# A four-layer network on one core: product with C on GpSimd, state sums by accumulating transfers, softmax reciprocals through DRAM

## The chip, the core and the metric

The kernel runs on one core of a Trainium2 chip. The metric is the device time of one execution in microseconds. Before the change it is 3715.52 us, the median of three runs (3714.67 to 3716.05). The profile is of one execution with a span of 3718.9 us.

Engine names are those of the profile: PE is TensorE (matrix products), PEld its weight loads, DVE is VectorE, ACT is ScalarE, POOL is GpSimd, and SP is SyncE, which issues nearly all transfers.

## What is computed

Four images of 128 channels and 64 x 64 pixels pass through four layers; N = 4096 is the number of pixels.

```python
# layer 0: attention over the pixels, 16 channels for q and k
energy = q^T k;  attn = softmax(energy);  x = gamma * (v @ attn^T) + x
# layer 1: two 3x3 convolutions with 4-bit weights and activations, residual
# layer 2: selective scan over the 4096 pixels, 256 inner channels, 16 states
def step(h, inp):
    dt_t, B_t, C_t, x_t = inp
    dA = exp(dt_t[..., None] * A)
    h = dA * h + dt_t[..., None] * B_t[:, None, :] * x_t[..., None]
    y = einsum('bdn,bn->bd', h, C_t)          # sum over the 16 states
    return h, y
# ys = scan(step) + xc * D; y = ys * silu(z); x = silu(group_norm(y @ W_out)) + x
# layer 3: attention over the pixels, 64 channels, softmax, output projection, residual
```

The change touches the sum over states in layer 2 (`y = einsum(h, C)`) and the division of both attentions by their softmax sums.

## The kernel before

All four layers run interleaved, so that each engine finds work in one layer while another waits. Each piece of work is a Python generator that yields `op(engine, time, needs...)` before it issues an instruction. `Order.run` (line 80) repeatedly takes the generator whose next operation could begin earliest by the planned times, adds a small penalty by rank (line 95), and lets it issue. The result is one fixed order of instructions for every engine and for the transfer queue. `lag` is the planned time from the issue of a transfer to its landing. An entry marked `port` is planned so as not to overlap another such entry, since DVE and GpSimd can hold each other up. The real waits on the chip are semaphores that the framework puts in; the plan only fixes the order.

**Attention (layers 0 and 3).** There are eight stages of 64 steps: layer 0 of images 0, 1 and 2, then layer 3 of image 0, layer 0 of image 3, and layer 3 of images 1, 2 and 3. In one step `t` PE computes energies `e` of 1024 keys against 256 queries (line 494), ACT takes the exponentials `p` (line 513), and PE multiplies them with the values into `us[:, 0]` (line 571) and with ones into `us[:, 1]`, which gives the softmax sums (line 591). In the first eight column blocks and in the last stage DVE adds the exponentials first (`acc`, line 535) and PE sums only the result. Four steps make one block of 256 queries in a single PSUM bank, `us`. PE opens each bank with products of zero (line 553), so that all later products may accumulate.

After two blocks (512 queries, a chunk; 64 chunks in all) `parts` lets ACT copy values and sums out (lines 617 and 619), and `finish` divides: four products with `sel4` turn the sums into columns (line 638), DVE takes reciprocals (line 647), four products with the identity spread them over all partitions (line 651), and DVE multiplies (line 659). In layer 0 the result is added into the padded image `xpad` (line 664); in layer 3 it is projected (line 670), added to the residual `o` loaded by `residual`, and written out (line 677).

**Scan (layer 2).** An image is cut into 8 pieces of 512 pixels; 32 pieces `g` with 16 states `n` make 512 steps `m`. Every tile of a step is 128 partitions x 1024 values (two halves of 256 channels). For each step:

- SP fetches the rows of B and C for state `n` from DRAM, broadcast to all partitions (`bc`, line 978, 512 KB, three buffers);
- ACT computes the decays `da` into PSUM (line 991, two halves);
- DVE multiplies `ud` with B into `hs` (line 1018, three buffers), runs two scans in place (line 1026), and then, after the next step's product with B, multiplies the state with C (`readout`, line 1008);
- ACT saves the last column for the next piece (`hlast`, line 1001);
- GpSimd adds the product to `y` (line 1043). After 16 states it multiplies `y` with the gate `sz` (line 1047), and PE projects it into `yo` (line 905).

`yo` of a whole image stays in SBUF in eight buffers until its group norm is known; then `x2` is formed in place and written to DRAM (line 969), from where layer 3 reads it (`stage_input`, line 378).

Of the kernel before, what the change touches and what calls it, by code (L numbers as in the profile page):

```python
# [8 lines left out]
F32 = mybir.dt.float32  # L9
# [11 lines left out]
P = 128  # L21
W = 64
N = W * W
TB = 512
# [23 lines left out]
class Order:  # L48
# [7 lines left out]
    def __init__(self):  # L56
        self.clock = dict.fromkeys(("PE", "ACT", "DVE", "POOL", "SP"), 0.0)
        self.marks = {}
        self.chains = []
        self.table = None  # L60
        self.bank = 0.0
        self.port = 0.0
        self.end = (0.0, None)

    @staticmethod
    def op(engine, time, *needs, bank=False, table=None, port=False, lag=0.0):
        return engine, time, needs, bank, table, port or engine == "POOL", lag
# [9 lines left out]
    def release(self):  # L77
        self.bank = self.end[0]

    def run(self):  # L80
        while self.chains:
            best = None
            for item in self.chains:
                engine, time, needs, bank, table, port, lag = item[3]
                if any(k not in self.marks for k in needs) or (bank and self.bank is None):
                    continue
# [3 lines left out]
                if bank:  # L90
                    start = max(start, self.bank + self.HOP)
# [8 lines left out]
            engine, time, needs, bank, table, port, lag = item[3]  # L100
# [3 lines left out]
            if bank:  # L104
                self.bank = None
# [29 lines left out]
def conv_seq_kernel(ctx: ExitStack, tc: tile.TileContext, i: dict, out: bass.AP):  # L135
# [47 lines left out]
    zero = const.tile([P, 1], BF16, tag="zero", name="zero")  # L183
    nc.gpsimd.memset(zero, 0.0)
# [49 lines left out]

    sel4 = const.tile([P, 1], F32, tag="sel4", name="sel4")
    nc.gpsimd.memset(sel4, 0.0)
    for k in range(4):
        nc.gpsimd.memset(sel4[32 * k : 32 * k + 1, :], 1.0)
# [126 lines left out]
    def stage_input(s):  # L365

        layer, b = stages[s]
        for c in range(NTB // 2):
            need = [("x2", b, 2 * c), ("x2", b, 2 * c + 1)] if layer == 3 else []
            need += [("sums", s * NS - 2 + c // 2), ("exp", s * NS - 1, 1)]  # L370
            yield op("SP", 0.1, *need, lag=3.5)
# [10 lines left out]
    def operands(s):  # L382
# [19 lines left out]
        def high_low(o, g, key, bias, low, n):  # L402
# [3 lines left out]
            yield op("ACT", 0.2 + n * 1e-3, (*key, "in"), *lows[c - 1 : c])  # L406
            h = att.tile([P, 2 * TB], F32R, tag="h", name="h", bufs=1)
            nc.scalar.activation(h[:, 0:n], g, AF.Identity, bias=low[1], scale=low[0])
            yield op("DVE", 0.06 + n * 1.2e-3)
            nc.vector.scalar_tensor_tensor(o, g, bias, h[:, 0:n], ALU.add, ALU.subtract)  # L410
            mark(*key)
# [4 lines left out]
        for c in range(NTB // 2):  # L416
# [9 lines left out]
            if layer == 0:  # L426
                order.add(1, high_low(o, flat(g), key, bq0r, low0[0], 2 * TB))
            else:
                order.add(1, copy(o, flat(g), key, 1.2))
# [24 lines left out]
            if layer == 0:  # L454
                mark(*key, "in")
                o = jts[s][:, c * TB : (c + 1) * TB]
                order.add(1, high_low(o, g[:, 0, :], key, bk0r, low0[1], TB))
# [15 lines left out]
            order.add(1, copy(o, flat(g) if layer == 0 else g, key, 1.2))  # L473
        return freed + lows

    def energies():
# [5 lines left out]
        for s, (layer, b) in enumerate(stages):  # L482
            if s:
                order.add(1, stage_input(s))
# [37 lines left out]
    def accumulations():  # L522
        for t in filter(added, range(len(stages) * NS)):
            k, q = divmod(t, NQ)
            for h in range(2):
# [6 lines left out]
                if q == 0:  # L532
                    accs[k] = att.tile([P, 2, 2, CB], F32, tag="acc", name="acc", bufs=1)
# [4 lines left out]
    def products():  # L538
        mark("evict", -1)
        for t in range(len(stages) * NS):  # L540
# [3 lines left out]
            for h in range(2):  # L544
                need = [("evict", k0 - 1)] if q == 0 and h == 0 else []
                time = (1.93 if layer == 0 else 0.95) + (0.3 if need else 0.0)
                yield op("PE", time, ("exp", t, h), *need)
                if need:

                    us = uss[k0] = ps_u.tile([P, 2, CB], F32, tag="us", name="us")  # L550
                    d = P if layer == 0 else 32
                    for m in range(P // d):
                        nc.tensor.matmul(
                            flat(us)[m * d : (m + 1) * d, :],
                            lhsT=w3[:, 0, m * d : (m + 1) * d],
                            rhs=zero.to_broadcast([P, TB]),
                            start=True,
                            stop=False,
                        )
                for k in range(2 * h, 2 * h + 6):  # L560
# [9 lines left out]
                    for rows, cols in tiles:  # L570
# [4 lines left out]
                            start=False,  # L575
# [26 lines left out]
    def parts():  # L602


        for s, (layer, b) in enumerate(stages):
            for c in range(NTB):
                k0 = s * NCB + 2 * c
                us = ss = None
                for k in range(k0, k0 + 2):
                    need = [("parts", s * NTB + c - 2)] if s or c > 1 else []  # L610
                    yield op("ACT", 0.45, ("sums", (k + 1) * NQ - 1), *need)
                    if us is None:
                        us = att.tile([P, TB], F32, tag="us", name="us", bufs=2)
                        ss = att.tile([P, TB], F32, tag="ss", name="ss", bufs=2)
                    cols = slice((k - k0) * CB, (k - k0 + 1) * CB)
                    scale = gam0 if layer == 0 else 1.0
                    nc.scalar.activation(us[:, cols], uss[k][:, 0, :], AF.Copy, scale=scale)
                    yield op("ACT", 0.4)
                    nc.scalar.copy(ss[:, cols], uss.pop(k)[:, 1, :])
                    mark("evict", k)  # L620
                if layer == 3:
                    order.add(1, residual(b, c))
                order.add(0, finish(s, c, us, ss))

    def residual(b, c):
        n = NTB * b + c
        yield op("SP", 0.1, *([("out", n - 1)] if n else []), lag=2.5)
        outs[b, c] = o = att.tile([P, TB], F32, tag="o", name="o", bufs=1)
        nc.sync.dma_start(out=o, in_=x2s[b][c])
        mark("res", n)  # L630

    def finish(s, c, us, ss):
        layer, b = stages[s]
        n = 2 * NTB * b + (0 if layer == 0 else NTB) + c
        yield op("PE", 0.65, bank=True)
        sc = gtile("sc")
        for k in range(4):
            nc.tensor.matmul(  # L638
                sc[:, k : k + 1],
                lhsT=ss[:, k * P : (k + 1) * P],  # L640
                rhs=sel4,
                start=True,
                stop=True,
            )
        yield op("DVE", 0.18)
        r = rall[:, 4 * n : 4 * n + 4]
        nc.vector.reciprocal(r, sc[:, 0:4])

        yield op("PE", 1.15)
        for k in range(4):  # L650
            nc.tensor.matmul(  # L651
                sc[:, k * P : (k + 1) * P],
# [897 lines left out]
```

## Time and profile before

| quantity | value |
|---|---|
| time, median of three runs | 3715.52 us |
| span of the profiled execution | 3718.9 us |
| mean TensorE clock granted | 0.967 |
| scan steps on DVE, first to last start | 242.9 to 3361.4 us |
| PE `us` products with values (L571), busy | 1521.7 us |
| PE energies (L494), busy, two row groups | 534.6 and 196.5 us |
| PE softmax sums with ones (L591), busy | 469.9 us |
| PE `sc` sums (L638), `sc` broadcasts (L651), zero products (L553), busy | 72.7, 74.5, 48.3 us |
| DMA queue of SP, share of 16 engines' span | 34.7% |

The span in 40 equal slices, busy tenths of each, shows how the work is spread; the scan fills slices 3 to 36:

```profile
PE   5999979989989999999888999999899989998998
DVE  3369999999999999899988999999789888893333
ACT  3467767777787777777677767767777777774443
POOL 0014434444434444344433444443344444441000
PEclk8999999999999999999999999999999999999999
DMA  2023334333443334443443333343434444331000
```

Transfers, with size and median time from issue to landing:

```profile
bc<-bc_d SPq DMA_DIRECT2D x512, 512.0 KB, 4.9
x_in<-in_x SPq DMA_DIRECT2D x16, 512.0 KB, 4.8
xpad<-in_x SPq DMA_DIRECT2D x32, 256.0 KB, 3.4
x_d<-yo SPq DMA_DIRECT2D x32, 256.0 KB, 2.3
x_in<-x_d SPq DMA_DIRECT2D x16, 512.0 KB, 6.0
o<-x_d SPq DMA_DIRECT2D x32, 256.0 KB, 5.4
out<-o SPq DMA_DIRECT2D x32, 256.0 KB, 2.2
bc_d<-xd SPq DMA_DIRECT2D x64, 32.0 KB, 1.7
```

### The profile page before, as it was taken

The page shows a single profiled execution, that of the slowest core. Times are in us where ns is not written, and L with a number is a line of the kernel's source. Part 1 is how long each engine was busy: PE and PEld are TensorE (multiplying, and loading weights), DVE is VectorE, ACT ScalarE, POOL GpSimd, SP SyncE. Part 2 cuts the span into 40 slices and gives each one's busy share as a digit, 9 for nine tenths or more (in the row PEclk, how much of TensorE's full clock was granted, in tenths as well). Part 3 has the DMA queues.
Part 4 walks back from the last instruction along what each step waited for, and adds up shares of the span by engine and source line. Part 5 has one row for each costly group of instructions (what it writes and reads, how often), then busy time and mean ns, then how long its engine had stood idle before and what let it go on. Part 6 is the DMA issues. An engine that isn't in the chain of part 4 may idle for free.

```text
span 3718.9 us, 70774 instructions
## 1 busy us (share of the span) xinstructions
PE 3406.0 (92%) x29874; PEld 2235.8 (60%) x29879; DVE 3104.3 (83%) x2944; ACT 2513.0 (68%) x3656; POOL 1314.1 (35%) x568
## 2 busy tenths in 40 slices
PE   5999979989989999999888999999899989998998
PEld 3776656666666666655545666665555545565665
DVE  3369999999999999899988999999789888893333
ACT  3467767777787777777677767767777777774443
POOL 0014434444434444344433444443344444441000
PEclk8999999999999999999999999999999999999999
DMA  2023334333443334443443333343434444331000
GB/s 70 1 53 96 91 103 100 90 95 92 117 102 97 94 87 95 112 107 101 106 114 102 89 91 92 88 112 87 107 95 108 119 91 108 101 104 63 13 19 17
DMA packets 203658, 327.82 MB, mean 88 GB/s; under 512 B 50609, under 2 KB 53441, under 8 KB 203329
## 3 DMA queue, kind: packets, MB, share of 16 engines
q1 hardware_dynamic: 196384, 322.09, 34.7%
q8 instruction: 236, 3.87, 0.4%
q10 hardware_dynamic: 6944, 1.10, 0.2%
q14 instruction: 94, 0.76, 0.1%
HBM read 304.27 MB, written 18.87 MB: 87 GB/s over the span
## 4 chain that ended last, share of the span: by engine, by line
PE 61%; DVE 21%; ACT 10%; issue 5%; DMA 2%; ACTq 0%; SPq 0%; DVEq 0%
PE us L571 25%; PE e L494 14%; DVE hs L1026 9%; PE us L591 7%; DVE hs L1018 4%; DVE hs L1008 3%; PE conv L686 2%; ACT da L991 2%; ACT p L513 2%; PE xh L775 2%; PE sc L651 2%; PE yo L905 1%; PE sc L638 1%; PE proj L465 1%; PE proj L423 1%
## 5 line engine op out<-in xcount | busy, mean ns | idle before, releaser
L1043 POOL TENSOR_TENSOR y<-y,hs 128x1024 f32<-128x1024 f32 x512 | 1215.3, 2374 | 2050.1 <-DVE hs L1008 2033.6
L571 PE MATMUL us<-p,v 128*32 128x256 f32 (+1 forms) x12288 | 1521.7, 389 | 128.3 <-ACT p L513 128.1
L571 PEld LDWEIGHTS us<-p,v 128*32 128x32 f32 (+1 forms) x12288 | 1009.0, 138 | 550.1 <-ACT p L513 153.5
L513 ACT ACTIVATE p<-e 128x1024 f32<-128x1024 f32 x1024 | 1002.0, 1019 | 383.2 <-PE e L494 255.5
L1026 DVE TENSOR_TENSOR_SCAN hs<-da,hlast,hs 128x512 f32<-128x512 f32 x896 | 1102.3, 1264 | 45.5 <-ACT da L991 45.2
L991 ACT ACTIVATE da<-dt,amat 128x512 f32<-128x512 f32 x1024 | 701.1, 690 | 266.8 <-DVE hs L1026 263.0
L1008 DVE TENSOR_TENSOR hs<-hs,bc 128x1024 f32<-128x1024 f32 x512 | 666.9, 1303 | 34.7 <-ACT hlast L1001 33.8
L1018 DVE TENSOR_TENSOR hs<-ud,bc 128x1024 f32<-128x1024 f32 x512 | 656.9, 1283 | 0.0
L494 PE MATMUL e<-it,v 64*128 64x256 f32 x4096 | 534.6, 402 | 9.2 <-ACT p L513 8.2
L494 PEld LDWEIGHTS e<-it,v 64*128 64x128 f32 x4096 | 386.9, 193 | 155.6 <-issue 89.6
L591 PE MATMUL us<-p,ones 128*32 128x256 f32 x7040 | 469.9, 385 | 0.0
L591 PEld LDWEIGHTS us<-p,ones 128*32 128x32 f32 x7040 | 202.4, 110 | 183.6 <-issue 64.5
L535 DVE TENSOR_TENSOR acc<-p 128x1024 f32<-128x1024 f32 x24 | 29.4, 1225 | 225.4 <-PE us L591 192.6
L494 PEld LDWEIGHTS e<-it,j 64*128 64x128 f32 x2048 | 141.5, 190 | 101.9 <-issue 69.1
L494 PE MATMUL e<-it,j 64*128 64x256 f32 x2048 | 196.5, 310 | 5.1 <-ACT p L513 3.4
L1001 ACT COPY hlast<-hs 128x2 f32<-128x2 f32 x448 | 85.4, 191 | 130.9 <-DVE hs L1026 129.1
L535 DVE TENSOR_TENSOR acc<-p,acc 128x1024 f32<-128x1024 f32 x96 | 117.4, 1223 | 61.6 <-ACT p L513 58.1
L1026 DVE TENSOR_TENSOR_SCAN hs<-da,hs 128x512 f32<-128x512 f32 x128 | 149.9, 1204 | 8.6 <-ACT da L991 8.5
L775 PEld LDWEIGHTS <-w 128*128 128x128 bf16 x576 | 51.4, 98 | 98.3 <-issue 54.3
L775 PE MATMUL xh<-x,w 128*128 128x512 fp8e4 x384 | 95.3, 385 | 1.1 <-ACT sz L798 0.4
L1047 POOL TENSOR_TENSOR y<-y,sz 128x1024 f32<-128x1024 f32 x32 | 95.2, 2976 | 2.5
L465 PE MATMUL proj<-L_conv_wvT,x_in 128*128 128x128 f32 (+1 forms) x512 | 67.7, 288 | 22.9 <-DVE it L410 13.2
(162 smaller groups left out, 2617.3 us busy)
## 6 DMA issues: line engine op xcount, KB each, us to landing
bc<-bc_d SPq DMA_DIRECT2D x512, 512.0 KB, 4.9
x_in<-in_x SPq DMA_DIRECT2D x16, 512.0 KB, 4.8
xpad<-in_x SPq DMA_DIRECT2D x32, 256.0 KB, 3.4
x_d<-yo SPq DMA_DIRECT2D x32, 256.0 KB, 2.3
x_in<-x_d SPq DMA_DIRECT2D x16, 512.0 KB, 6.0
o<-x_d SPq DMA_DIRECT2D x32, 256.0 KB, 5.4
out<-o SPq DMA_DIRECT2D x32, 256.0 KB, 2.2
bc_d<-xd SPq DMA_DIRECT2D x64, 32.0 KB, 1.7
```

Source lines behind the costliest of these rows:

```text
L465: nc.tensor.matmul(to[:, k * d : (k + 1) * d], lhsT=x[:, k // 4, k % 4 * P : (k % 4 + 1) * P], rhs=wv, start=True, stop=True,)
L494: nc.tensor.matmul(e[k % 4 // 2][:, k % 2, k // 4, :], lhsT=jts[s][row : row + D3, col : col + P], rhs=its[s][row : row + D3, c * CB : (c ...
L513: nc.scalar.activation(p, es[t][h], AF.Exp)
L535: nc.vector.tensor_add(accs[k], ps[t, h], other)
L571: nc.tensor.matmul(us[rows, 0, :], lhsT=vts[s][:, 8 * q + k, cols], rhs=ps[t, h][:, k % 2, k // 4, :], start=False, stop=False,)
L591: nc.tensor.matmul(us[32 * m : 32 * m + 32, 1, :], lhsT=ones[:, 0:32], rhs=term, start=False, stop=q == NQ - 1 and k >= len(terms) - 4,)
L775: nc.tensor.matmul(g, lhsT=w3[:, k // len(rhs), lhs[k % len(rhs)] : lhs[k % len(rhs)] + P], rhs=x[:, rhs[k % len(rhs)]], start=(k == 0), s ...
L991: nc.scalar.activation(da, live["in", g][0][:, h, :], AF.Exp, scale=amat[:, h, n : n + 1])
L1008: nc.vector.tensor_mul(hs, hs, bcs.pop(m)[:, 1:2, :].to_broadcast([P, 2, TB]))
L1018: nc.vector.tensor_mul(hs, ud, bcs[m][:, 0:1, :].to_broadcast([P, 2, TB]))
L1026: nc.vector.tensor_tensor_scan(hs[:, h, :], das.pop((m, h)), hs[:, h, :], hlast[:, n, h : h + 1] if g % NTB else 0.0, ALU.mult, ALU.add,)
L1043: nc.gpsimd.tensor_tensor(y, y, hss.pop(m), ALU.add)
```

## The change

**Product with C and sum over states.** GpSimd, not DVE, multiplies the state with C. It then issues a transfer that adds the product into one of three tiles in SBUF: `y`, `odd1` or `odd2`, by `n % 3`. The transfers of states 1 and 2 overwrite `odd1` and `odd2`, all others add. After 16 states DVE adds `odd1` and `odd2` into `y`, and GpSimd multiplies with the gate as before. `hs` and `bc` have four buffers each instead of three. DVE is to be relieved of one of its two products per step.

**Softmax reciprocals.** ACT copies values and sums out in one instruction. The sums go to DRAM (`s_d`), come back as 128 partitions x 4 x 4 (`st`), DVE reduces and inverts them, the reciprocals go to DRAM (`r_d`) and come back broadcast to all partitions (`rb`). DVE multiplies with `rb`. PE's products with `sel4` and the identity go away. `rb` shares one buffer with the residual `o`, whose load now waits for the product.

**Opening of the bank.** The first product of a bank carries the start flag, so the products of zero go away.

**Buffers.** To make room, `yo` goes to DRAM and comes back in two batches of four, `h` shares the buffer `sp` with the softplus, and `acc` shares `odd1`.

**Plan.** The planned transfer times are raised (for example `bc` from 5.0 to 7.5 us, an accumulating transfer is planned at 8.2), and the ranks of the generators are set anew. In the plan a GpSimd operation no longer takes the port by default, since issuing a transfer does not.

```diff
@@ class Order
-        return engine, time, needs, bank, table, port or engine == "POOL", lag
+        return engine, time, needs, "bank" if bank else lock, table, port, lag
@@ accumulations
-                    accs[k] = att.tile([P, 2, 2, CB], F32, tag="acc", name="acc", bufs=1)
+                    accs[k] = pair("acc", "odd1", 1).rearrange("p a (b c) -> p a b c", b=2)
@@ products
-                    d = P if layer == 0 else 32
-                    for m in range(P // d):
-                        nc.tensor.matmul(
-                            flat(us)[m * d : (m + 1) * d, :],
-                            lhsT=w3[:, 0, m * d : (m + 1) * d],
-                            rhs=zero.to_broadcast([P, TB]),
...
-                            start=False,
+                            start=q == 0 and k < (1 if layer == 0 else 2),
@@ parts
-                    yield op("ACT", 0.45, ("sums", (k + 1) * NQ - 1), *need)
+                    yield op("ACT", 0.6, ("sums", (k + 1) * NQ - 1), *need)
...
-                    nc.scalar.activation(us[:, cols], uss[k][:, 0, :], AF.Copy, scale=scale)
-                    yield op("ACT", 0.4)
-                    nc.scalar.copy(ss[:, cols], uss.pop(k)[:, 1, :])
+                    nc.scalar.copy(us[:, :, k - k0, :], uss.pop(k))
@@ finish
-        yield op("PE", 0.65, bank=True)
-        sc = gtile("sc")
...
-        nc.vector.tensor_mul(us, us, sc)
+        yield op("SP", 0.1, ("evict", 2 * k + 1), lag=5.0)
+        s_d = dram.tile([4, TB], F32, tag="s_d", name="s_d")
+        nc.sync.dma_start(out=s_d, in_=us[0:P:32, 1, :])
+        us = us[:, 0, :]
+        mark("s_d", k)
+        yield op("SP", 0.1, ("s_d", k), lag=7.0)
+        st = att.tile([P, 4, 4], F32, tag="st", name="st", bufs=2)
+        nc.sync.dma_start(out=st, in_=s_d.rearrange("g (p e) -> p g e", e=4))
+        mark("st", k)
+        yield op("DVE", 0.3, ("st", k))
         r = rall[:, 4 * n : 4 * n + 4]
+        nc.vector.tensor_reduce(r, st.rearrange("p g e -> p e g"), AX.X, ALU.add)
+        nc.vector.reciprocal(r, r)
+        yield op("SP", 0.1, lag=5.0)
+        r_d = dram.tile([TB], F32, tag="r_d", name="r_d")
+        nc.sync.dma_start(out=r_d.rearrange("(p e) -> p e", e=4), in_=r)
+        mark("r_d", k)
+        yield op("SP", 0.1, ("r_d", k), *([("end", k - 1)] if k else []), lag=8.0)
+        rb = att.tile([P, TB], F32, tag="o", name="rb", bufs=1)
+        nc.sync.dma_start(out=rb, in_=r_d.unsqueeze(0).to_broadcast([P, TB]))
...
+        nc.vector.scalar_tensor_tensor(us, us, scale, rb, ALU.mult, ALU.mult)
@@ output
-            yo = big.tile([P, TB], F32, tag="yo", name="yo", bufs=NTB)
+            yo = big.tile([P, TB], F32, tag="yo", name="yo", bufs=4)
...
+            nc.sync.dma_start(out=yo_d[c], in_=yo)
...
+                    x2.append(big.tile([P, TB], F32, tag="yo", name="x2", bufs=4))
+                    nc.sync.dma_start(out=x2[-1], in_=yo_d[k])
@@ fetches
-            need = [("c", m - 3)] if m > 2 else []
-            yield op("SP", 0.1, ("bc_d", g), *need, lag=5.0)
+            need = [("c", m - 4)] if m > 3 else []
+            yield op("SP", 0.1, ("bc_d", g), *need, lag=7.5)
@@ scans
-            if m:
-                yield op("DVE", 1.22, ("last", m - 1), port=True)
-                readout(m - 1)
@@ additions becomes readouts and gates
-            yield op("POOL", 2.36, ("c", m), ("y", g))
-            nc.gpsimd.tensor_tensor(y, y, hss.pop(m), ALU.add)
+            yield op("POOL", 2.6, ("s", m, 1), ("last", m), port=True)
+            nc.gpsimd.tensor_tensor(
+                hs, hs, bcs.pop(m)[:, 1:2, :].to_broadcast([P, 2, TB]), ALU.mult
+            )
...
+            need = [("y", g)] if n == 0 else [("add", m - 3)] if n > 2 else []
+            if n in (1, 2) and g:
+                need.append(("summed", g - 1, n))
+            yield op("POOL", 1.2, *need, lag=8.2)
...
+            nc.gpsimd.dma_start(
+                out=sums[g][n % 3],
+                in_=hss.pop(m),
+                accum_op=ALU.bypass if n in (1, 2) else ALU.add,
+            )
...
+                yield op("DVE", 1.22, ("add", m - 4 + k), ("add", m - 1), port=True)
+                nc.vector.tensor_add(y, y, sums[g][k])
@@ ranks
-            (3, scans()),
-            (3, additions()),
-            (3, fetches()),
+            (1, scans()),
+            (6, readouts()),
+            (-1, gates()),
+            (8, fetches()),
```

## The prediction

> **What bounds the kernel now.** I read the busy shares first, then the same shares for the stretch in which the state scan of layer 2 runs (248 to 3348 us), because the kernel opens and closes without it.
>
> ```profile
> PE 3406.0 (92%) x29874; PEld 2235.8 (60%) x29879; DVE 3104.3 (83%) x2944; ACT 2513.0 (68%) x3656; POOL 1314.1 (35%) x568
> ...
> PE 61%; DVE 21%; ACT 10%; issue 5%; DMA 2%; ACTq 0%; SPq 0%; DVEq 0%
> ```
>
> The first line is busy time, the second the engines' shares of the chain that ended last. TensorE (PE) leads both, but a fifth of the chain runs over VectorE (DVE). Busy time by stretch (columns: length, PE, PEld, DVE, ACT, POOL, granted clock, DMA share, GB/s) shows why:
>
> ```profile
> 248.00:3348.00 3100.00, 2859.35 (x24465) 1868.90 (x24470) 2875.16 (x2650) 2237.44 (x3330) 1298.69 (x539) 0.97 0.40 100
> 3392.00:3719.00 327.00, 313.25 (x3777) 196.66 (x3777) 110.70 (x109) 143.99 (x169) 0.00 (x0) 0.98 0.07 23
> ```
>
> In the scan's 3100 us PE is busy 92.2% and DVE 92.7%: two engines at their limit, each making the other wait. In the last 327 us, where attention runs alone, PE is 96% busy and DVE 34%. So work has to leave both engines to shorten the middle; only PE's counts at the end. The groups of instructions price it (busy us, mean ns):
>
> ```profile
> L1043 POOL TENSOR_TENSOR y<-y,hs 128x1024 f32<-128x1024 f32 x512 | 1215.3, 2374 | 2050.1 <-DVE hs L1008 2033.6
> L1026 DVE TENSOR_TENSOR_SCAN hs<-da,hlast,hs 128x512 f32<-128x512 f32 x896 | 1102.3, 1264 | 45.5 <-ACT da L991 45.2
> L1008 DVE TENSOR_TENSOR hs<-hs,bc 128x1024 f32<-128x1024 f32 x512 | 666.9, 1303 | 34.7 <-ACT hlast L1001 33.8
> L1018 DVE TENSOR_TENSOR hs<-ud,bc 128x1024 f32<-128x1024 f32 x512 | 656.9, 1283 | 0.0
> ```
>
> One state step (512 of them) is on DVE a product with B (L1018), a product with C (L1008) and two scans: 1.28 + 1.30 + 2.5 = 5.1 us, while a step has 3100/512 = 6.05 us on average. GpSimd waits 2034 us for the product with C.
>
> **What the Trainium skill says.** "GPSIMD Engine Reference", section 3.1, gives about 2.6 cycles an element for a two-input operation on GpSimd; by that page's 1.2 GHz clock 1024 elements take 2.22 us, an estimate. The trace agrees: 2.37 us with its overhead. "SBUF — State Buffer", section "SBUF: two separate sides", says that a DVE operation with two SBUF inputs and a GpSimd operation that reads SBUF take one port pair exclusively; the later one blocks. The trace shows it in the timeline (start, length):
>
> ```profile
> 1511.73 3.22 POOL L1047 TENSOR_TENSOR y<-y,sz 128x1024 f32<-128x1024 f32 x1
> ...
> 1512.65 3.38 DVE L1008 TENSOR_TENSOR hs<-hs,bc 128x1024 f32<-128x1024 f32 x1
> ```
>
> The DVE product, 1.21 us when free, took 3.38 us behind a GpSimd product. "DMA: Bandwidth & Descriptors", section "SWDGE vs HWDGE vs iDMA", says that accumulating transfers can be issued by GpSimd alone and share the 16 DMA engines with all others; its "Rules for kernel authors" say that an accumulate reads its destination and writes it later, so the next one on the same bytes must wait for it. No run here shows an accumulate yet.
>
> **The change part by part.**
>
> *Product with C from DVE to GpSimd.* DVE loses 512 x 1.30 = 667 us. GpSimd pays 512 x 2.37 us for it (the L1043 row, same shape), but loses the 512 additions of the same price: even.
>
> *Sums by transfers.* The y addition becomes an accumulating transfer of 512 KB per step. Issuing: not in the trace; low the 0.36 us that an SP issue of this shape takes, high the 1.2 us that the diff plans; I take 1.2. GpSimd then needs 2.37 + 1.2 = 3.6 us a step, and up to 1.3 us more when the product with B holds the port: 4.9 us at worst, under 6.05. Three destinations rotate (y, odd1, odd2), so a transfer may take three steps before the next on its tile is held. What is queued behind a held issue on GpSimd is the next product with C, then through four hs buffers the product with B. The loop of one hs buffer is 1.28 + 2.5 + 0.2 + 2.37 + 1.2 + L over 4 steps; it reaches 6.05 us a step only at L = 16.6 us. The diff plans 8.2; the plain bc transfer of the same size lands in 4.9. Folding odd1 and odd2 into y costs DVE 64 x 1.22 = 78 us.
>
> *DMA engines.*
>
> ```profile
> q1 hardware_dynamic: 196384, 322.09, 34.7%
> ```
>
> 322 MB took 34.7% of 3719 us = 1290 us, so 0.524 MB takes 2.1 us of all engines. An accumulate costs between that and, with two reads for one, twice that: 2.1 to 4.2 us. With the bc fetch a step needs 4.2 to 6.3 us. I take 3.2, also what the skill's fit ("Anatomy of one DMA", 2.0 us + bytes/436e3, an estimate) gives: 5.3 us, hidden under PE but close. The fourth bc buffer pays for slower fetches.
>
> *Softmax reciprocals and zero products off PE.* Timeline durations: sc sums 0.61 us, sc broadcasts 1.16 us per 512 columns, zero products 0.39 us per 256 columns, so 64 x (0.61 + 1.16 + 0.78) = 163 us of PE, all removed: 138 us in the middle (54 of 64 chunks), 25 outside. DVE's reciprocal stays, with a small reduce in front (64 x 0.2 = 13 us) and the product from SBUF instead of PSUM (+0.06 each). ACT's two copies, 0.47 or 0.38 plus 0.37 us, become one planned at 0.6: about -25 us in all. The replacement is four transfers in a row. Behind them waits only DVE's us product; PE needs its result only for the next image row block, and the us buffer is free for two chunks, some 100 us (16 t-steps at about 6). Hidden, except once: at the end.
>
> *The end.* Now 3704.9 (last sum) to 3718.9 = 14 us. Afterwards s_d, st, r_d, rb, residual and out follow each other: with lightly loaded landings from the rows of small transfers (1.7 to 3.4 us each) about 16 us, plus 9 us of engine work and hops: 25. Cost 11 us.
>
> *yo through DRAM, sp buffers shared with h, residual later.* 32 x 256 KB out and back, on queues with room; the attention inputs wait for it, hidden if the scan runs ahead of PE, otherwise some 20 us for each of the four images. I take 0 and put up to 80 us in the range.
>
> *New planning figures and ranks.* They reorder the queues; nothing is computed differently. 0, with the risk in rival A.
>
> **The sum.** DVE in the middle: 2875 - 667 + 78 + 13 = about 2300 us, no longer a limit. PE there: 2859 - 138 = 2721 us. With DVE out of the way PE's share should lie between today's 92.2% and the 96% of the last stage; I choose 95%: 2721/0.95 = 2864 us, 236 less than 3100. Then 3716 - 236 - 20 (outside, rounded down from 25 for idle time left) + 11 = 3471; I say **3470**.
>
> **The rivals.** *A: PE sheds the work but not the waits.* The order in every queue is fixed, and more transfers whose landing varies (bc 3.5 to 9.1 us in the trace) sit in it; one late landing holds everything behind it on SP or GpSimd. For it: PE's own waits today are mostly on exponentials (us on p: 128 us for PE, 153 for its loads), not on DVE directly. Share kept at 92.2%: 2721/0.922 = 2951, so 3716 - 149 - 20 + 11 = 3558, and with the 80 us of yo waits 3640. Against it: stretches of 124 us in which layer 0 attention runs already have PE at 97%.
>
> *B: the transfers become the bound, slower than before.* At 6.3 us a step: 512 x 6.3 = 3226; the scan starts at 240 and about 357 us follow it: 240 + 3226 + 357 = 3823. For it: DMA share in the middle is 40% now and would reach 90 to 100%. Against it: it needs the high price of the accumulate.
>
> *C: PE packs as in its best stretches* (97%): 2721/0.97 = 2805, 3716 - 295 - 20 + 11 = 3412, with a few us off the end 3390.
>
> **How the numbers follow.** Forecast (3400 to 3530) 0.50; A (3530 to 3700) 0.27; C (under 3400) 0.05; B 0.18, of it 0.01 near no change. Faster 0.81, same 0.02, slower 0.17. The range runs from C's 3390 to A's upper end with another 60 us of late landings, 3700; it leaves out B.
>
> **What would show it.** Right: DVE's busy share in the middle near 75 to 80%, PE 94 to 96%, no sc or zero groups, the GpSimd product with C near 2.4 us, accumulates landing below 12 us, DVE at a tenth of the chain or less. Wrong: DMA share over 85% with scans waiting for hs or bc (B); GpSimd products of 3.5 us or more, blocked at the port; PE still at 92% with waits on transfers in the list of waits (A); PE idle ahead of the layer 3 stages while x_in lands.

## The result and the profile after

The changed kernel takes **3698.15 us** (median of four runs, 3695.66 to 3701.16) against 3715.78 us before (3714.67 to 3719.82). The ratio is 0.9951, 95% interval 0.9934 to 0.9968: 18 us faster where 246 were forecast.

From the page of the changed kernel (busy time; a DMA queue; the shares of the chain that ended last; two groups; landings):

```profile
PE 3286.2 (89%) x28535; PEld 2117.5 (57%) x28535; DVE 2899.9 (78%) x2560; ACT 2479.3 (67%) x3529; POOL 1872.9 (51%) x1074
...
q0 software_dynamic: 73728, 268.47, 34.7%
...
PE 28%; DVE 21%; issue 19%; POOL 17%; DMA 10%; ACT 5%; POOLq 0%; SPq 0%; DVEq 0%; ACTq 0%
...
L1032 POOL TENSOR_TENSOR hs<-hs,bc 128x1024 f32<-128x1024 f32 x512 | 1394.5, 2724 | 1184.7 <-ACT hlast L996 1077.4
...
L1008 DVE TENSOR_TENSOR hs<-ud,bc 128x1024 f32<-128x1024 f32 x512 | 773.7, 1511 | 36.5 <-DMA bc<-bc_d 25.9
...
odd<-hs POOLq DMA_DIRECT2D x320, 512.0 KB, 7.7
y<-hs POOLq DMA_DIRECT2D x192, 512.0 KB, 8.0
```

PE's share of the chain fell from 61% to 28%, and DVE kept its 21%: the scan's loop over DVE, GpSimd and ACT limits more often than before, PE less often. The product with B (L1008), which the change doesn't touch, went from 1283 to 1511 ns. Busy time in the scan's stretch and at the end (length, PE, PEld, DVE, ACT, POOL, clock, DMA share, GB/s):

```profile
248.00:3348.00 3100.00, 2786.48 (x23731) 1785.18 (x23728) 2691.08 (x2273) 2227.65 (x3254) 1865.30 (x1054) 0.95 0.81 196
3392.00:3698.00 306.00, 282.48 (x3528) 174.05 (x3526) 111.62 (x117) 139.38 (x150) 0.00 (x0) 0.97 0.10 23
```

DVE lost a product of 667 us and is only 184 us less busy (2875 to 2691). PE sits at 89.9% instead of 92.2%. By the starts of the products with B, the scan lasts 3080 us instead of 3114 (-33), starts at 262.0 instead of 242.9 (+19), and 356 instead of 362 us follow its last step (-6): together -20, the difference of the two spans.

The timeline shows what fills DVE (start, length):

```profile
1169.20 3.56 DVE L1008 TENSOR_TENSOR hs<-ud,bc 128x1024 f32<-128x1024 f32 x1
...
1169.31 2.36 POOL L1032 TENSOR_TENSOR hs<-hs,bc 128x1024 f32<-128x1024 f32 x1
```

A product with B that takes 1.20 us when free (its median) starts within 0.11 us of a GpSimd product with C and ends 1.09 us after it.

The prediction said that the later one blocks, and so it is in this trace: of 63 products with B that start up to 1.5 us behind a product with C, 62 are held (over 1.6 us; 3.13 us in the mean); of 231 that start 0.12 to 0.8 us ahead of one, 5 are, and it is the product with C that takes 2.91 us in the mean, instead of 2.36. Closer than 0.12 us the recorded starts don't tell: the product shown starts 0.11 us ahead and is held.

Two sums over the traces measure this. **Blocked time**: for every DVE instruction between 260 and 3340 us, what it took above the tenth percentile of its kind. It was 151 us before and is 411 now. **Neighbours**: what DVE ran beside GpSimd's 512 additions (before) or products with C (after). Before, 86% of GpSimd's time lay beside scans and 6.6% beside products with B; now it is 46% and 25%. The experiments ask whether this is the cause, and whether it is the use of the port (the pair that, by the prediction, DVE and GpSimd hold against each other) as such or its place in the step.

### The profile page after: what moved, and what is told of

It is laid out like the page before. It is cut to its first block, busy times and chain, and to the rows that moved or that the text cites. A ratio compares the mean times of both kernels' runs of the same rounds, so it can differ in the third digit from the quotient of the medians.

```text
span 3698.5 us, 69437 instructions
## 1 busy us (share of the span) xinstructions
PE 3286.2 (89%) x28535; PEld 2117.5 (57%) x28535; DVE 2899.9 (78%) x2560; ACT 2479.3 (67%) x3529; POOL 1872.9 (51%) x1074
## 4 chain that ended last, share of the span: by engine, by line
PE 28%; DVE 21%; issue 19%; POOL 17%; DMA 10%; ACT 5%; POOLq 0%; SPq 0%; DVEq 0%; ACTq 0%
PE us L556 13%; POOL hs L1032 13%; DVE hs L1014 8%; PE e L488 7%; DVE hs L1008 7%; DMA bc<-bc_d 3%; PE us L576 3%; POOL odd L1042 2%; DMA odd<-hs 2%; DMA y<-hs 2%; ACT p L507 1%; DVE ud L869 1%; POOL y L1058 1%; PE conv L670 1%; POOL y L1042 1%
## 5 line engine op out<-in xcount | busy, mean ns | idle before, releaser
L1032 POOL TENSOR_TENSOR hs<-hs,bc 128x1024 f32<-128x1024 f32 x512 | 1394.5, 2724 | 1184.7 <-ACT hlast L996 1077.4
L1008 DVE TENSOR_TENSOR hs<-ud,bc 128x1024 f32<-128x1024 f32 x512 | 773.7, 1511 | 36.5 <-DMA bc<-bc_d 25.9
L1042 POOL DMA_DIRECT2D odd<-hs x320 | 263.3, 823 | 192.3 <-DVE y L1055 90.9
L1042 POOL DMA_DIRECT2D y<-hs x192 | 169.5, 883 | 62.9 <-POOL hs L1032 60.5
L599 ACT COPY us<-us 128x512 f32<-128x512 f32 x128 | 74.7, 584 | 78.8 <-PE us L576 77.3
L459 PE MATMUL proj<-L_conv_wvT,x_in 128*128 128x128 f32 (+1 forms) x512 | 75.8, 310 | 57.2 <-DVE it L403 47.5
```

Source lines behind the costliest of these rows:

```text
L1008: nc.vector.tensor_mul(hs, ud, bcs[m][:, 0:1, :].to_broadcast([P, 2, TB]))
L1032: nc.gpsimd.tensor_tensor(hs, hs, bcs.pop(m)[:, 1:2, :].to_broadcast([P, 2, TB]), ALU.mult)
L1042: nc.gpsimd.dma_start(out=sums[g][n % 3], in_=hss.pop(m), accum_op=ALU.bypass if n in (1, 2) else ALU.add,)
```

## The experiments

Times are medians; "changed" stands for the changed kernel (3698.15 us). The kernels e3, e4, e5, e6, e9 and e10 keep the planned order of every queue of the changed kernel, e12 that of the kernel before; the others let the plan run anew, so that small differences of theirs can also come from another order.

| run | edit | us | ratio to before (95%) |
|---|---|---|---|
| e1_softmax | before, softmax part alone | 3711.08 | 0.9983 to 1.0001 |
| e2_scan | changed, softmax part undone | 3747.55 | 1.0071 to 1.0105 |
| e3_small_adds | changed, small transfers | 3639.41 | 0.9788 to 0.9832 |
| e4_half_product | changed, half product with C | 3527.32 | 0.9485 to 0.9517 |
| e5_half_filled | e4, write-only fills added | 3559.51 | 0.9563 to 0.9597 |
| e6_half_small | e3 and e4 together | 3476.56 | 0.9343 to 0.9377 |
| e7_split | halves on DVE and GpSimd | 3952.80 | 1.0620 to 1.0658 |
| e8_half_softmax_on_pe | e4, softmax part undone | 3583.85 | 0.9637 to 0.9673 |
| e9_two_products | product with C in two | 3676.17 | 0.9874 to 0.9917 |
| e10_four_products | product with C in four | 3879.49 | 1.0425 to 1.0459 |
| e11_old_plan | old ranks and planned times | 3889.14 | 1.0452 to 1.0487 |
| e12_before_two_adds | before, addition in two | 3745.24 | 1.0063 to 1.0096 |
| e13_first_on_pe | first three chunks divided on PE | 3755.46 | 1.0090 to 1.0124 |
| e14_plan_port | five conv operations planned as port | 3701.39 | 0.9953 to 0.9981 |
| e15_alternate | every second product with C on DVE | 3709.77 | 0.9978 to 0.9998 |
| e15b_quarter | every fourth product with C on DVE | 3682.27 | 0.9898 to 0.9935 |
| **e16_copy_after** | hlast copied by DVE after the next product with B | **3474.53** | 0.9332 to 0.9377 |
| e17_copy_before | the same copy before that product | 3870.11 | 1.0402 to 1.0437 |

### What GpSimd's product costs

```diff
 e4_half_product
-            nc.gpsimd.tensor_tensor(hs, hs, <C of bc>, ALU.mult)
+            nc.gpsimd.tensor_tensor(hs[:, 0, :], hs[:, 0, :], bcs.pop(m)[:, 1, :], ALU.mult)
 e5_half_filled, in addition
+            for _ in range(2):
+                nc.gpsimd.memset(bc[:, 0, :], 0.0)
```

> The changed kernel with GpSimd's product with C on the first 512 of 1024 columns only (the other half is summed without C); transfers and order are unchanged. If the port held by the product is what delays VectorE (411 us above its shortest durations in the scan's stretch): 3560 to 3640, with the product with B back near 1.2 us mean. If transfers hold it: within 15 us of the changed kernel. If the fixed order does: 3670 to 3700.

> The changed kernel with GpSimd's product on half the columns (half of the states are summed without C), followed by two GpSimd fills of 512 columns of the dead B half of the bc tile, which only write SBUF. GpSimd is as long busy per step as in the changed kernel, but reads through the shared port for half as long. If the port is what costs: about 3530 to 3570, as with the half product alone (3527). If GpSimd's own time per step, and with it the length of the loop over the buffers, is what costs: 3680 to 3720.

The groups of e4, then of e5:

```profile
L1032 POOL TENSOR_TENSOR hs<-hs,bc 128x512 f32<-128x512 f32 x512 | 815.0, 1592 | 1480.1 <-ACT hlast L996 1246.7 <-DVE hs L1014 129.1 <-DVE rall L627 28.8
L1008 DVE TENSOR_TENSOR hs<-ud,bc 128x1024 f32<-128x1024 f32 x512 | 673.8, 1316 | 54.9 <-DMA bc<-bc_d 47.1 <-DMA odd<-hs 3.8 <-issue 3.6
```

```profile
L1008 DVE TENSOR_TENSOR hs<-ud,bc 128x1024 f32<-128x1024 f32 x512 | 686.9, 1342 | 51.3 <-DMA bc<-bc_d 38.4 <-issue 4.9 <-DMA odd<-hs 3.2
L1035 POOL MEMSET bc<- 128x512 f32 x1024 | 549.9, 537 | 29.5
```

Half a product is worth 171 us. In e5 the fills bring GpSimd's busy time back (808 + 550 us against 1394), but only 32 of the 171 us: DVE's product with B stays at 1342 ns, blocked time at 215 us (e4: 186). So some 139 us are not GpSimd's time but what its product does to DVE while it reads; that the port is the way there is argued from the blocked time (411 to 186). The small effect of the fills agrees with the Trainium skill, "SBUF — State Buffer", section "Who interferes with whom": a DVE instruction with two SBUF inputs contends with a GpSimd instruction that reads SBUF, not with one that only writes it.

### What the transfers cost

```diff
 e3_small_adds (e6_half_small: on top of e4)
+            if n not in (1, 2):
+                dst, src = dst[:, 0, 0:P], src[:, 0, 0:P]
```

> The changed kernel with the accumulating transfers of states 0 and 3 to 15 cut to 128 of 1024 columns (most of the sum over states is left out); the order of instructions is unchanged. If load on the DMA engines or late landings hold the scan: 3550 to 3640, DMA share in the scan's stretch near 0.5. If GpSimd's product at the port holds it: within 15 us of the changed kernel. If the fixed order alone does: within 15 us too.

> The changed kernel with both the half product and the small accumulating transfers (most of the sum over states and half of the products with C left out). If port and transfers cost separately, the gains of 171 and 59 us add: about 3470. If both relieve the same wait: 3515 to 3530. If TensorE is the limit once the port is relieved: not under 3450.

With 14 of 16 accumulates cut to an eighth, the DMA share of the middle falls from 0.81 to 0.56 and the time by 59 us; on top of the half product, by 51. The two gains nearly add: e6 is 222 us under the changed kernel, its scan 2860 us long. DVE's blocked time in e3 stays at 404 us, so the transfers don't cause it. Nor does their issuing on GpSimd: in e16 (below) 143 products with B run beside an issue and no GpSimd product, and take 1.22 us in the mean, 1.21 with neither beside them.

### What the softmax part brings

e1 makes only that part of the change (start flag, one copy by ACT, reciprocals through DRAM) on the kernel before; e2 and e8 undo it in the changed kernel and in e4; e13 leaves the first three chunks on PE.

```diff
 e13_first_on_pe
+        if s == 0 and c < 3:
+            ...  # sums with sel4, reciprocal, broadcast with ident, as before
+        else:
             ...  # through s_d, st, r_d, rb
```

> The kernel before with only the softmax part: start flag in place of the zero products, sums and reciprocals through DRAM, one eviction copy. The scan keeps its product with C on VectorE and its additions on GpSimd. If the two parts simply add and the softmax part brings what the prediction gave it (163 us less TensorE work, but VectorE stays at 93% in the scan's stretch), about 3640 to 3670. If TensorE time is not what sets the pace while VectorE is full: 3690 to 3720. If the transfers through SyncE's queue cost more than they save: above 3720.

> The changed kernel with the softmax part undone: zero products, softmax sums and reciprocals on TensorE as before; the scan part stays. If the softmax transfers and their waits are what ate the gain: faster than the changed kernel, 3600 to 3680. If the scan part itself is what does not pay: the added TensorE work makes it slower than before, 3750 to 3850. If TensorE work is hidden behind another limit: the same as the changed kernel, 3690 to 3710.

> The half product of GpSimd (half of the states summed without C) with the softmax part undone, so that TensorE again makes sums, broadcasts and zero products. If TensorE is the limit once the port is relieved, the full 163 us come back: 3660 to 3690. If they come back as in the changed kernel, where undoing the part cost 49 us: 3560 to 3590.

> The changed kernel with the softmax sums and reciprocals of the first three chunks of image 0 on TensorE as before, all others through DRAM. If the four transfers in a row delay the first convolution and with it the scan: the scan starts near 243 us instead of 262, and the time is 15 to 20 us shorter, about 3680. If the scan catches up elsewhere: the same as the changed kernel within 5 us.

Alone it brings 4 us, an interval that includes none. PE only runs out of attention work sooner: in e1 no product with values starts for 118 us from 3302.9, ahead of the last stage, against 40 us from 3378.5 before the change. Beside the scan part it brings 49 us (e2 against changed), with the half product 57 (e8 against e4). Nearly all of that lies behind the scan: e2's scan starts 17 us sooner and lasts 18 us longer than the changed kernel's, but 403 us instead of 356 follow its last product with B; in e8 it is 401 against 354, with a scan 37 us longer and a start 20 us sooner. PE has attention left over there (busy for 93 us before the last stage starts in e2, for 30 in the changed kernel). The part costs 19 us at the opening: the scan starts at 262 us in e1 and in the changed kernel, at 245 in e2, at 242.0 in e13 and at 242.9 before. Yet e13 is a miss: the new order lost more in the scan than the start gained. Its products with B start from 242.0 to 3406.1, 6.19 us a step instead of 6.03, and 28% of GpSimd's time lies beside them.

### A shorter hold, or less of it

```diff
 e9_two_products (e10: four pieces of 256; e12: the addition of before in two)
+            for h in range(2):
+                nc.gpsimd.tensor_tensor(hs[:, h, :], hs[:, h, :], bc[:, 1, :], ALU.mult)
 e7_split: DVE, after the next product with B; GpSimd multiplies the other half
+        nc.vector.tensor_mul(hs[:, 1, :], hs[:, 1, :], bcs[m][:, 1, :])
 e15_alternate: m % 2 == 1 (e15b_quarter: m % 4 == 3) is multiplied by DVE, there
+        nc.vector.tensor_mul(hs, hs, bcs.pop(m)[:, 1:2, :].to_broadcast([P, 2, TB]))
```

> The changed kernel with GpSimd's product with C in two instructions of 512 columns; the result is complete, and the planned order is unchanged. [...]If how long one GpSimd instruction holds the port is what costs: VectorE's blocked time falls from 411 us to some 250, and the time to 3580 to 3650. If the port's total use is what costs, or the fixed order: 3690 to 3720.

> The same in four instructions of 256 columns, about 0.7 us each. If the length of one hold is what costs: a little faster again than two, 3550 to 3630, unless GpSimd, which then gives way to VectorE more often, becomes late itself: 3650 to 3720.

> The kernel before with GpSimd's addition to y in two instructions of 512 columns; the result is complete. If the port also costs in the kernel before (VectorE is 151 us above its shortest durations there): 3660 to 3700. If GpSimd's addition lies beside the scans, which use no port: 3705 to 3725.

> The product with C split: VectorE multiplies the second half of the columns, after the next step's product with B, GpSimd the first half; the result is complete. Port time per step falls from 1.2 + 2.4 to 1.2 + 0.65 + 1.25 us, VectorE gets 0.65 us more per step. If the port is what costs: between the half product (3527) and the changed kernel, 3540 to 3620. If VectorE's load costs as much as the port's: 3680 to 3720.

> The product with C of every other state on VectorE, after the next step's product with B as in the kernel before, the rest on GpSimd; all sums by accumulating transfers; the result is complete. Port time per step falls from 3.6 to about 3.0 us, VectorE gets 0.6 us more per step. If the port's total use is what costs: 3580 to 3650. If VectorE's load then takes over: 3690 to 3740.

> The same with one state in four on VectorE: port time 3.3 us per step, VectorE 0.3 us more. If the port's total use is what costs: between the changed kernel and the alternating one, 3620 to 3670. If VectorE's load takes over: 3690 to 3720.

If the length of one hold were the cost, two holds of half the length should have relieved DVE. Blocked time was 408 us in e9 (411 whole) and 613 in e10. DVE is not let in between the halves: of the 105 products with B that e9 holds over 1.6 us, 50 run beside both halves and end about 1.1 us behind the second, like the one at 500.65 us (3.49 us; the halves run from 500.26 to 503.05). e9's gain of 22 us has another cause, not settled. In e12 the two half additions are longer together (1290 against 1215 us), reach into the next product with B (9.7% instead of 6.6%), and cost 30 us. In e7 the copy releases GpSimd's half 0.40 us behind the start of the next product with B. That product holds it, so that it takes 1.92 us, and it then holds DVE's half, which starts 0.72 us later (all medians). e7, e10 and e12 are slower than any of their expectations allowed. The groups of e7:

```profile
L1041 POOL TENSOR_TENSOR hs<-hs,bc 128x512 f32<-128x512 f32 x512 | 922.0, 1801 | 1124.7 <-ACT hlast L996 1106.5 <-DVE hs L1008 9.5 <-DVE hs L1017 4.3
L1031 DVE TENSOR_TENSOR hs<-hs,bc 128x512 f32<-128x512 f32 x512 | 701.3, 1370 | 36.0 <-ACT hlast L996 36.0
```

DVE's half takes 0.66 us at its shortest and 1.37 in the mean. e15 halves GpSimd's products and takes blocked time down to 190 us, but 256 products of 1.2 us on DVE (312 us) take DVE's time instead; with one in four the time is 16 us under the changed kernel's.

### What the plan does

e14 marks five single-source operations of the convolutions as `port` in the plan, since they too became slower (together 96 us before and 165 now; the one on L725 went from 746 to 1211 ns). e11 gives the changed kernel the ranks and planned transfer times of before.

```diff
 e14_plan_port
-                yield op("DVE", 0.43)
+                yield op("DVE", 0.43, port=True)
 e11_old_plan
-            yield op("SP", 0.1, ("bc_d", g), *need, lag=7.5)
+            yield op("SP", 0.1, ("bc_d", g), *need, lag=5.0)
...
-            (6, readouts()),
+            (1, readouts()),
```

> The changed kernel with VectorE's five single-source operations of the convolutions marked as users of the port in the plan; nothing but the order changes. If what the port costs comes from an order that does not know these operations (100 us above their shortest durations): 3630 to 3670. If the total use of the port sets it: 3680 to 3710.

> The changed kernel with the ranks of before, and with the planned times of before for the transfers that existed then (bc 5.0, images 3.5, stores 2.5 us); new transfers keep theirs. If the measured transfer times and ranks matter: slower than the changed kernel, 3750 to 3850. If they are hidden by the port: 3690 to 3720.

e14 changes nothing, and the five operations still take 165 us. e11 costs 191 us, more than expected, with less blocked time (344 us) and more idle time on DVE (590 us against 398, between 260 and 3340 us). So the new ranks and times are no by-work: the changed kernel is worse without them. Which of them matters was not taken apart.

### The place in the step

Before, GpSimd's addition was released by DVE's product with C, right ahead of the two scans. Now the product with C is released by ACT's copy `hlast`, that is by the end of the scans, just when DVE turns to the next product with B. Two kernels move that release. Against each other they differ in nothing but the place of the copy: both traces show the same instructions in the same order on every engine. Against the changed kernel they also differ in the plan, which ran anew, and in the engine of the copy. DVE makes the copy in place of ACT; the product with C overwrites the copied columns, so it follows the copy.

```diff
 e16_copy_after (in scans, behind the product with B of step m)
+            if m:
+                yield op("DVE", 0.1)
+                nc.vector.tensor_copy(hlast[:, (m - 1) % DS, :], hss[m - 1][:, :, TB - 1])
+                mark("last", m - 1)
             for h in range(2):
                 ...  # the scans
 e17_copy_before: same plan, but the copy of step m is issued right behind its own scans
```

> The changed kernel, but the last columns of a step's state (hlast, 512 copies of 128x2) are saved by DVE instead of ACT, right after the NEXT step's product with B. The product with C overwrites these columns, so it is now released when the product with B has ended, and runs beside the next two scans. In the trace of the changed kernel GpSimd's products with C spend 25% of their time beside DVE's product with B and 46% beside scans; before the change GpSimd's additions spent 6.6% beside the product with B and 86% beside scans. Theory 'place in the step' (the port costs DVE so much because the product with C is released at the very moment at which DVE turns to its next two-input operation): overlap with the product with B falls under 8%, its mean from 1511 to about 1300 ns, DVE's blocked time in the middle from 411 to about 250 us, less about 40 us for the copies: 3560 to 3630 us. Theory 'use of the port' (only the time for which GpSimd reads counts, wherever it lies): 3690 to 3760 us, with the copies' 40 us on DVE.

> As the other kernel of this pair, with the same order in every queue, except that DVE saves the last columns BEFORE the next product with B, right after the step's second scan, so that the product with C is again released just as the product with B starts. Theory 'place in the step': overlap with the product with B 25% or more, its mean 1500 ns or more, 80 to 150 us slower than the other kernel of the pair. Theory 'use of the port': within 30 us of it.

3474.53 and 3870.11 us, **396 us apart** by the place of a 128x2 copy: the theory of the place holds, with more than twice the difference that was expected of it. Of the 224 us between the changed kernel and e16 a part can be the new order. Sums over the traces:

| | before | changed | e16 | e17 |
|---|---|---|---|---|
| GpSimd's 512 operations of the step, busy us | 1215 | 1394 | 1218 | 1480 |
| beside scans | 86% | 46% | 86% | 33% |
| beside products with B | 6.6% | 25% | 1.3% | 42% |
| DVE blocked, us | 151 | 411 | 134 | 594 |
| ACT's decays wait for the scans, us | 263 | 314 | 238 | 675 |

In e17 125 products with B start up to 1.5 us behind a product with C, and all are held; in the changed kernel there were 63 of these, in e16 2. The groups of e16 and of e17:

```profile
L1031 POOL TENSOR_TENSOR hs<-hs,bc 128x1024 f32<-128x1024 f32 x512 | 1218.3, 2379 | 1140.7 <-DVE hlast L992 1119.5 <-DVE rall L626 7.4 <-ACT xh L692 1.6
...
L1001 DVE TENSOR_TENSOR hs<-ud,bc 128x1024 f32<-128x1024 f32 x512 | 626.8, 1224 | 68.7 <-DMA bc<-bc_d 43.2 <-issue 11.7 <-DMA odd<-hs 10.5
```

```profile
L1030 POOL TENSOR_TENSOR hs<-hs,bc 128x1024 f32<-128x1024 f32 x512 | 1479.6, 2890 | 1246.7 <-DVE hlast L992 1170.2 <-DVE rall L626 69.7 <-DVE rs_v L237 5.9
...
L1001 DVE TENSOR_TENSOR hs<-ud,bc 128x1024 f32<-128x1024 f32 x512 | 972.3, 1899 | 2.8 <-DMA bc<-bc_d 1.8 <-issue 0.8
```

And a step of e16 in the timeline, with nothing blocked (in brackets the idle time before it and its releaser):

```profile
1500.22 1.23 DVE L1001 TENSOR_TENSOR hs<-ud,bc 128x1024 f32<-128x1024 f32 x1
...
1501.36 0.16 DVE L992 COPY hlast<-hs 128x2 f32<-128x2 f32 x1
1501.55 2.46 DVE L1011 TENSOR_TENSOR_SCAN hs<-da,hlast,hs 128x512 f32<-128x512 f32 x2
1501.61 2.36 POOL L1031 TENSOR_TENSOR hs<-hs,bc 128x1024 f32<-128x1024 f32 x1 [0.45 <-DVE hlast L992]
```

The product with C, 2.36 us, fits beside the two scans, 2.46 us. That scans beside it keep their price (those with `hlast` take 1270 ns where it runs beside them for over 90% of their time, 1274 where no product runs) agrees with the same section of "SBUF — State Buffer", by which a DVE instruction with at most one SBUF input, outside its 2-port modes, doesn't contend: a scan's decays come from PSUM. Relief of ACT is not the reason, since e17 has it too. e16's page:

```profile
PE 3204.8 (92%) x28535; PEld 2076.1 (60%) x28535; DVE 2656.6 (77%) x3072; ACT 2433.5 (70%) x3081; POOL 1740.9 (50%) x1074
...
PE 56%; POOL 13%; issue 10%; DMA 9%; DVE 6%; ACT 5%; POOLq 0%; ACTq 0%; SPq 0%; DVEq 0%
```

DVE is down to 6% of the chain. e16 does all of the computation and is the fastest kernel that does, 6.5% under the kernel before.

## Why the prediction was wrong

The time, 3698 us, lies just inside the far end of the range (3700); of the forecast gain of 246 us 18 came.

- **Co-bound middle: right.** Relief of PE alone (e1) brought 4 us.
- **"DVE in the middle about 2300 us, no longer a limit": the step that failed.** It came to 2691. Over the whole run DVE's busy time was to fall by 576 us (667 - 78 - 13) and fell by 204. The product with C is gone and the two folds cost 78 us, as forecast. Left out, above all, was that DVE's other work would become dearer, by 307 us in all: product with B +117 us, ud with y +45 (39 to 84), the five single-source operations of the convolutions +70, and so on. The other 65 us or so are an overlap: durations of neighbours on DVE overlap (before, they add up to 3285 us where DVE is busy for 3104), so a product taken out frees less than its own length. The prediction quoted the rule of the port and a DVE product blocked for 3.38 us, and then priced the block for GpSimd only ("up to 1.3 us more").
- **"Product with C from DVE to GpSimd ... even": right in time, wrong in place.** GpSimd's load is the same kind and nearly the same length. But the prediction didn't ask what DVE does at the moment of release. Between e16 and e17 this alone is worth 396 us.
- **GpSimd's step of 3.6 us: right, by luck.** It measured 2.72 + 0.85 (issues of 0.82 and 0.88 us) = 3.6 us: the 1.2 us for an issue was 0.35 too high, and the product was blocked by as much. Under 6.05, as forecast. GpSimd's own time still cost up to 32 us for half a product (e5), which was priced at nothing.
- **Transfers "hidden": wrong by some 50 us.** An accumulate took less of the engines than assumed, 0.347 x 3698.5 / 512 = 2.51 us against 3.2, and landed in 7.7 to 8.0 us, under the 12 named. (The 3.2 leaned on a fit for the time of one transfer, which is not its load on the engines; as a landing time it is far too short here.) Cutting them still brought 51 to 59 us. Rival B's sign, a share over 85%, was not met (0.81).
- **PE -163 us: mis-sized, and the clock left out.** The `sc` sums were taken at 0.61 us per chunk, but busy time gives 72.7/64 = 1.14, so the three lines that went were worth 196 us. Yet PE's busy time fell by only 120 (3406 to 3286), at a granted clock of 0.949 instead of 0.967. The same 28535 matmuls take 3205 us in e16 at 0.973 and 3327 in e17 at 0.943. Busy time multiplied by the clock is 3293 before, 3119 after, 3117 in e16 and 3136 in e17 (the lowest of the kernels with the same matmuls is 3070, in e7 and e15), so some 175 us of work at full clock went, and the lower clock took a third of it back. PE's idle time between 260 and 3340 us rose from 241 to 307 us, so that 95% became 90%. Whether the lower clock cost time, or only came with the waits, was not tested. In e16 PE is busy 94.2% of 248 to 3120 us.
- **Softmax transfers "hidden, except once": they show twice.** At the end as forecast (from the last sum to the end of the span 14 us before, 26 after; 25 forecast), and 19 us at the opening, which the prediction missed.
- **yo through DRAM at 0:** not tried by itself; it is in all kernels derived from the changed one, e16 among them.
- **Rival A** named a PE share that stays because of waits, but put them on late transfers. Small transfers brought 59 us (e3); another place of the product, in a new order, brought 224 (e16).

With the release moved, the forecast's sum nearly holds: by the products with B e16's scan is 270 us shorter than before (2844 against 3114) where 236 were worked out, and the kernel takes 3474.5 us where 3470 were. Part of this agreement is luck: PE lost 201 us of busy time, not 163, while DVE's copies took 110 us and the scan started 23 us later, neither of which was in the sum.

## What to carry to other kernels

When work moves to an engine that shares a port with another, price the block for both sides, and look up what each of them is doing at the moment when the moved instruction is released: beside the scans the same instruction held up almost nothing (134 us of blocked time in e16, 594 in e17). The release can be placed by a small true dependency, here a copy whose columns the instruction overwrites, queued behind the work it should avoid. When two engines both limit a stretch, read from the trace whether one engine's freed time is really free before counting the other's.

## What the runs showed of the hardware

- Of a GpSimd product and a two-input DVE product, the one that starts later waits: 62 of 63 against 5 of 231 in the changed kernel. A held DVE product ends some 1.1 us behind the end of the GpSimd product.
- Cutting GpSimd's instruction into halves didn't relieve DVE, which waited for both: 408 us blocked against 411, four pieces 613.
- GpSimd fills that only write (537 ns for 128x512) moved DVE's two-input product from 1316 to 1342 ns. The single-source operation on L725 went from 695 to 870 ns in that kernel, which agrees with "Who interferes with whom" in "SBUF — State Buffer", by which such operations (`tensor_scalar`) can enter DVE's 2-port modes and then contend with GpSimd.
- Issuing an accumulating transfer took GpSimd 0.82 to 0.88 us and left DVE's product with B at 1.22 us (1.21 without).
- DVE's copy of 128x2 took 215 ns in the mean, ACT's 190.
